# Quarter products, seven for eight, in the adjacency sweeps of a four-layer graph kernel

**The chip, the cores and the metric.** One core of one Trainium2 chip. The metric is device microseconds of one execution, as the median of the runs. A single core has no die to compare with, so a run is called fast when it is within 1.5% of the fastest of its kernel. In the profile's lines PE is TensorE's matmuls and PEld its weight loads, DVE is VectorE, ACT ScalarE, POOL GpSimd, and SPq the queue of SyncE, which issues loads; L102 is line 102 of that kernel.

## The reference

2708 nodes, 512 features, a dense f32 array `adj` that is mostly zeros. Four layers, each with a residual and a layer norm. Cut to what matters:

```python
# 0: inc = adj + mask / sqrt(row count of mask)
x = LN(x + (inc @ x) / rowsum(inc))
# 1: attention over adj's pattern, and a GCN, mixed by two gates
e = where(adj != 0, exp(-leaky_relu(s_left[:, None] + s_right[None, :])), 0)
x = LN(x + sigmoid(gate_a * (e / rowsum(e)) @ (x @ W_sa) + gate_b * (adj @ (x @ W_gcn) + b)))
# 2: three hops
x = LN(x + x W0 + A (x W1 + A (x W2 + A (x W3))))
# 3: pooled
x = LN(x + relu((((A x + x) / deg) + x) @ W + b))
```

So there are seven products of the form `adjacency @ features`, [2708 x 2708] by [2708 x 512].

## The kernel before

The adjacency lies transposed in DRAM. Its 128 x 128 blocks are the stationary operand, and 512 features move. All features stay in SBUF.

```python
def sweep_mm(ps, lhs, rhs, m, q, first=True, last=True):
    w = rows[m]
    k0, k1 = PIECES[q]
    for k in range(k0, k1):
        kr = rows[k]
        nc.tensor.matmul(ps[:w], lhs[q][:kr, k - k0, :w], rhs[k][:kr], start=first and k == 0,
                         stop=last and k == NT - 1)
```

The scale of layer 0's mask is a column of one row tile: a power on GpSimd, then a transpose on PE that spreads it.

```python
nc.vector.tensor_scalar(r[:w, 0:1], ps[:w], 1.0, None, ALU.max)
nc.gpsimd.tensor_tensor(r[:w, 1:2], r[:w, 0:1], neg_half[:w], ALU.pow)
# ... later
nc.tensor.transpose(r[:, 0, :w], scale[m][:w, 1:2].to_broadcast([w, P]), ident[:w, :w])
```

A hop is a sweep over a row tile and four dense matmuls for `x W` into the same PSUM bank; `x` is transposed again in each hop.

## Time and profile before

3712.6 us (3711.8 to 3713.6, three runs). The prediction below shows the page's shares, slices and chain.

### The profile page before, as it was taken

The page shows a single profiled execution, that of the slowest core. Times are in us where ns is not written, and L with a number is a line of the kernel's source. Part 1 is how long each engine was busy: PE and PEld are TensorE (multiplying, and loading weights), DVE is VectorE, ACT ScalarE, POOL GpSimd, SP SyncE. Part 2 cuts the span into 40 slices and gives each one's busy share as a digit, 9 for nine tenths or more (in the row PEclk, how much of TensorE's full clock was granted, in tenths as well). Part 3 has the DMA queues.
Part 4 walks back from the last instruction along what each step waited for, and adds up shares of the span by engine and source line. Part 5 has one row for each costly group of instructions (what it writes and reads, how often), then busy time and mean ns, then how long its engine had stood idle before and what let it go on. Part 6 is the DMA issues. An engine that isn't in the chain of part 4 may idle for free.

```text
span 3710.3 us, 25433 instructions
## 1 busy us (share of the span) xinstructions
PE 3679.8 (99%) x10340; PEld 1626.9 (44%) x10340; DVE 1057.5 (29%) x1807; ACT 265.2 (7%) x392; POOL 88.8 (2%) x249
## 2 busy tenths in 40 slices
PE   7999999999999999999999999999999999999999
PEld 3444444444444444344444434444344444344443
DVE  6676654444444444110000000000000001222222
ACT  0000001111111111110000000000000000000000
POOL 0000000000000000000000000000000000000000
PEclk9999999999999999999999999999999999999999
DMA  4222211111111110102222122222222221222220
GB/s 149 53 56 56 54 44 55 31 34 30 33 30 30 30 33 19 37 24 60 60 60 60 48 71 60 60 60 60 59 60 60 60 60 48 77 69 71 68 71 21
DMA packets 377865, 197.16 MB, mean 53 GB/s; under 512 B 27156, under 2 KB 368364, under 8 KB 377748
## 3 DMA queue, kind: packets, MB, share of 16 engines
q1 hardware_dynamic: 370278, 181.58, 18.8%
q10 hardware_dynamic: 7470, 13.95, 1.1%
q8 instruction: 82, 1.34, 0.1%
q14 instruction: 35, 0.29, 0.0%
HBM read 189.94 MB, written 5.55 MB: 53 GB/s over the span
## 4 chain that ended last, share of the span: by engine, by line
PE 99%; DMA 1%; DVE 0%; issue 0%; POOLq 0%; SPq 0%
PE acc L102 68%; PE ps_u L102 11%; PE acc L116 9%; PE ps_d L116 6%; PE ps_t L109 2%; PE ps_s L129 1%; PE ps_s L171 1%; PE ps_s L284 1%; PE ps_s L210 0%; DMA adj<-in_adjT 0%; DMA w<-in_w_hop 0%; PE ps_t L262 0%; PE ps_u L186 0%; DMA A<-in_x 0%; DVE tmp L192 0%; DVE y L380 0%
## 5 line engine op out<-in xcount | busy, mean ns | idle before, releaser
L102 PE MATMUL acc<-C,adj 128*128 128x512 f32 (+2 forms) x1936 | 855.4, 595 | 0.0
L102 PE MATMUL acc<-B,adj 128*128 128x512 f32 (+2 forms) x1936 | 853.5, 594 | 0.0
L102 PEld LDWEIGHTS acc<-B,adj 128*128 128x128 f32 (+2 forms) x1936 | 352.5, 186 | 462.3 <-issue 461.1
L102 PEld LDWEIGHTS acc<-C,adj 128*128 128x128 f32 (+2 forms) x1936 | 352.2, 186 | 462.7 <-issue 462.1
L102 PE MATMUL acc<-A,adj 128*128 128x512 f32 (+1 forms) x968 | 436.1, 600 | 2.3 <-DVE adj L194 2.3
L102 PE MATMUL acc<-C,edge 128*128 128x512 f32 (+1 forms) x968 | 436.0, 597 | 0.0
L102 PE MATMUL ps_u<-B,adj 128*128 128x512 f32 (+1 forms) x968 | 434.6, 595 | 0.0
L116 PE MATMUL acc<-w,xT 128*128 128x512 f32 (+1 forms) x704 | 324.7, 604 | 1.4 <-DMA w<-in_w_hop 1.4
L102 PEld LDWEIGHTS acc<-C,edge 128*128 128x128 f32 (+1 forms) x968 | 176.0, 185 | 248.0 <-issue 248.0
L111 ACT COPY xT<-ps_t 128x512 f32<-128x512 f32 (+1 forms) x154 | 87.7, 570 | 2748.9 <-PE ps_t L109 2741.6
L102 PEld LDWEIGHTS ps_u<-B,adj 128*128 128x128 f32 (+1 forms) x968 | 176.6, 186 | 229.3 <-issue 229.2
L102 PEld LDWEIGHTS acc<-A,adj 128*128 128x128 f32 (+1 forms) x968 | 174.2, 187 | 214.1 <-issue 195.6
L116 PE MATMUL ps_d<-w,xT 128*128 128x512 f32 (+1 forms) x528 | 243.5, 604 | 0.5 <-DVE y L380 0.5
L116 PEld LDWEIGHTS acc<-w,xT 128*128 128x128 f32 (+1 forms) x704 | 124.4, 186 | 182.6 <-issue 180.9
L358 DVE COPY C<-acc 128x512 f32<-128x512 f32 (+1 forms) x22 | 15.2, 692 | 494.2 <-PE acc L116 494.2
L358 DVE COPY B<-acc 128x512 f32<-128x512 f32 (+1 forms) x22 | 15.2, 691 | 494.2 <-PE acc L116 494.2
L116 PEld LDWEIGHTS ps_d<-w,xT 128*128 128x128 f32 (+1 forms) x528 | 92.8, 186 | 129.9 <-issue 128.4
L361 DVE TENSOR_TENSOR y<-acc,A 128x512 f32<-128x512 f32 (+1 forms) x22 | 15.2, 692 | 413.6 <-PE acc L116 413.4
L131 DVE TENSOR_SCALAR rd<-ps_s 128x1 f32<-128x1 f32 (+1 forms) x44 | 6.9, 157 | 431.2 <-PE ps_s L129 431.2
L122 DVE TENSOR_REDUCE part<-edge 128x128 f32<-128x768 f32 (+3 forms) x88 | 111.6, 1305 | 0.0
L122 DVE TENSOR_REDUCE part<-adj 128x128 f32<-128x768 f32 (+3 forms) x88 | 111.6, 1309 | 0.0
L372 DVE TENSOR_SCALAR edge<-adj 128x768 bf16<-128x768 f32 (+3 forms) x88 | 44.2, 509 | 208.4 <-PE ps_s L171 152.1
(72 smaller groups left out, 1477.5 us busy)
## 6 DMA issues: line engine op xcount, KB each, us to landing
adj<-in_adjT SPq DMA_DIRECT2D x252, 384.0 KB
adj<-in_adjT SPq DMA_DIRECT2D x126, 320.0 KB
adj<-in_adjT SPq DMA_DIRECT2D x126, 256.0 KB
A<-in_x ACTq DMA_DIRECT2D x21, 256.0 KB
out<-xa SPq DMA_DIRECT2D x21, 256.0 KB
w<-in_w_hop ACTq DMA_DIRECT2D x4, 1024.0 KB
adj<-in_adjT SPq DMA_DIRECT2D x126, 10.0 KB
w<-in_w_sa ACTq DMA_DIRECT2D x1, 1024.0 KB
```

Source lines behind the costliest of these rows:

```text
L102: nc.tensor.matmul(ps[:w], lhs[q][:kr, k - k0, :w], rhs[k][:kr], start=first and k == 0, stop=last and k == NT - 1)
L109: nc.tensor.transpose(ps[:, c, :w], src[:w, c * P : (c + 1) * P], ident[:w, :w])
L111: nc.scalar.copy(t[:, :, :w], ps[:, :, :w])
L116: nc.tensor.matmul(ps[:w], xT[:, c, :w], wt[:, c, :], start=first and c == 0, stop=c == DC - 1)
L122: nc.vector.tensor_reduce(s[:, :w], t[:, :nk, :w].rearrange("p k i -> p i k"), AX.X, ALU.add)
L129: nc.tensor.matmul(ps[:w], s[:, :w], ones, start=n == 0, stop=n == len(parts) - 1)
L131: nc.vector.tensor_scalar(rd[:w], ps[:w], eps, None, ALU.add)
L171: nc.tensor.matmul(ps[:w], mask[m][q][:, k - k0, :w], ones_bf, start=k == 0, stop=k == NT - 1)
L284: nc.tensor.matmul(pz[:w], xT[m][:, c, :w], wab_sb[:, c, :], start=c == 0, stop=c == DC - 1)
L358: nc.vector.tensor_copy(dst[m][:w], ps[:w])
L361: nc.vector.tensor_tensor(y[:w], ps[:w], x2[m][:w], ALU.add)
L372: nc.vector.tensor_scalar(t[:, : k1 - k0, :w], adj[m][q][:, : k1 - k0, :w], 0.0, None, ALU.not_equal)
```

## The change

Each adjacency is split into 2 x 2 quarters of 1354 rows and columns, each feature matrix into 2 x 2 quarters of 1354 rows and 256 features. Seven products of sums of quarters replace eight. Features become the stationary operand and adjacency rows move, 256 to 384 at a time, so the result comes out transposed. The rows of `x W` in a hop become two more contraction tiles of the sweep. Features now travel through DRAM between sweeps, and the order of everything is given by positions. The diff has 1161 lines; its core (comments and dots are mine):

```diff
-        nc.tensor.matmul(ps[:w], lhs[q][:kr, k - k0, :w], rhs[k][:kr], ...)
+STAT = dict(P1="B11", P7="T3", P5="T1", P6="T2", P2="B21", P4="T4", P3="B22")
+MOV = dict(P1="11", P7="s3", P5="21", P6="11", P2="12", P4="22", P3="12")
+            cw = {"s3": 0.3, "s1": 1.1, "s2": 2.1, "s4": 5.05}          # when the sums of pieces are made
+                nc.vector.tensor_tensor(A[r, dst, k][:w, :n], A[r, a, k][:w, :n], A[r, b, k][:w, :n], op)
+                for c in range(2):
+                    nc.tensor.matmul(B[home, c][:, :n], X[STAT[p], k][:w, c * P : (c + 1) * P],
+                                     A[r, MOV[p], k][:w, :n], start=bool(start and k == k0), stop=k == k1, ...)
 ... (cut)
-        nc.gpsimd.tensor_tensor(r[:w, 1:2], r[:w, 0:1], neg_half[:w], ALU.pow)
+    def count_row(R0, n, h):
+        t = trans("cr")
+        nc.vector.tensor_scalar(t[:, :n], cnt.pop(h)[:, :n], 1.0, None, ALU.max)
+        row[R0, h] = ring_tile("row")
+        nc.gpsimd.tensor_tensor(row[R0, h][:, :n], t[:, :n], neg_half.to_broadcast([P, n]), ALU.pow)
+    def prep0(r, R0, n, h, hj, k, a):                                   # adjacency piece -> inc piece
+        nc.vector.scalar_tensor_tensor(t[:w, :n], a[:w, :n], 0.0, row[R0, h][:w, :n], ALU.is_gt, ALU.mult)
+        nc.vector.tensor_tensor(a[:w, :n], a[:w, :n], t[:w, :n], ALU.add)
+        add_run(R0, h, n, w, a)
 ... (cut)
```

Adjacency rows now lie along the free dimension, so the mask's scale is wanted as a row of 256 to 384 elements, the same on all partitions.

## The prediction

> **What bounds the kernel now.** I first read the header of the page and the busy shares, then the slices, then the chain that ended last.
>
> ```profile
> span 3710.3 us, 25433 instructions
> PE 3679.8 (99%) x10340; PEld 1626.9 (44%) x10340; DVE 1057.5 (29%) x1807; ACT 265.2 (7%) x392; POOL 88.8 (2%) x249
> PE   7999999999999999999999999999999999999999
> DVE  6676654444444444110000000000000001222222
> PEclk9999999999999999999999999999999999999999
> PE 99%; DMA 1%; DVE 0%; issue 0%; POOLq 0%; SPq 0%
> ```
>
> PE idles 30 us in all (3710.3 - 3679.8), 22 of them before the first sweep matmul, and the mean granted clock is 0.999. So the time is the sum of PE's matmuls. VectorE has work in the first third and then almost none. To price a matmul I took the timeline of PE in a stretch of a hop (start, length, engine, line, operation, count):
>
> ```profile
> 1810.43 3.70 PE L116 MATMUL acc<-w,xT 128*128 128x512 f32 x8
> 1813.97 10.46 PE L102 MATMUL acc<-B,adj 128*128 128x512 f32 x24
> 1824.27 0.60 PE L109 MATMUL ps_t<-ident,A 128*128 128x128 f32 x4
> 1824.71 5.74 PE L102 MATMUL acc<-B,adj 128*128 128x512 f32 x13
> ```
>
> 24 records run from 1813.97 to 1824.27: 0.429 us each, start to start; four transposes take 0.44 us. Each f32 matmul leaves two records (a row tile has 22 blocks and shows 44), so one 512-column f32 matmul costs 0.858 us. The same reading elsewhere gives 0.112 us per record where only 1 or 2 columns move, and 0.025 us for a bf16 count matmul with one column. For VectorE I took its timeline in layer 0:
>
> ```profile
> 212.00 0.94 DVE L192 TENSOR_TENSOR tmp<-edge,ps_u 128x768 f32<-128x768 bf16 x1
> 212.85 1.82 DVE L194 TENSOR_TENSOR adj<-adj,tmp 128x768 f32<-128x768 f32 x2
> 200.16 0.75 DVE L200 SCALAR_TENSOR_TENSOR y<-acc,rd,A 128x512 f32<-128x512 f32 x1
> 200.94 0.69 DVE L137 BATCH_NORM_STATS2 st<-y 128x6 f32<-128x512 f32 x1
> ```
>
> Two independent f32 adds of 768 columns take 1.82 us where one takes 0.95: the second follows after 0.87[...]. One that needs the result of the one before starts 0.03 us after its end (200.16 + 0.75, then 200.94)[...].
>
> [...]
>
> **The sweeps, PE.** Before: 7 products with the adjacency in 6 streams (layer 1 does two), 22 x 22 matmuls of 512 columns each: 3388 x 0.858 = 2907 us. In addition blocks of 20 rows cost some 0.1 us more per record (0.533 and 0.517 against 0.429) and so does one neighbour, 0.29 us x 154 row tiles = 44 us. After: a quarter product has 11 tiles of contraction (10 of 128, one of 74 rows), two halves of 128 features as stationary, and 1354 adjacency rows as moving columns in pieces of 384, 384, 256 and 330. One (tile, half) over the four pieces: [...] 2275 ns. 7 products x 22 = 154 of these per sweep, 350.4 us, against 415 + 6. Seven sweeps: 2453 us, 498 less. Only 8/7 of that is the algorithm; the rest is that 2708 rows are no longer padded to 22 full tiles on both sides. [...]
>
> **Hops' dense rows.** Removed: 3 x 22 x 4 matmuls, 264 x 0.858 = 227 us. Added: two more contraction tiles per quarter, 3 x 7 x 4 x 2275 ns = 191 us.
>
> **The rest of PE.** Unchanged in number: 352 dense matmuls (302 us), 616 transposes (67 us at 0.109; those saved by recomputing x2's once are spent on turning results back), 176 gate matmuls (39 us). Row sums fall from 176 matmuls to 44 (39 to 10 us). Degrees: 484 one-column counts remain (12 us); layer 0's become 176 matmuls with 338 columns on average, 143 ns each, 25 us for 12.
> Sum after: 2453 + 191 + 302 + 67 + 39 + 10 + 12 + 25 = 3099 us. The same sum for before is 2907 + 44 + 529 + 67 + 39 + 39 + 24 + 6 (wide transposes) = 3655; with 30 us idle, 3685 against a span of 3710, 0.7% short. Scaled by 3680/3655, after has 3120 us of PE work. With before's idle that would be 3150, 15% off; what remains is how much more PE will wait.
>
> **Where PE will wait.** By widths 384, 384, 256, 330 an independent f32 operation costs VectorE 420 ns on average, a chained one 535. Each sweep gets 176 sums of adjacency pieces (74 us), 11 x 4 sums of features (17), 40 additions that leave PSUM (18): 109 us, harmless beside 425 to 460 us of PE. Two sweeps have element work besides. Layer 0: 176 pieces x (two chained + one independent) = 176 x 1.49 = 262 us, layer norm with its waits on GpSimd 22 x 4.1 = 90, small ones 6: 467 us, against PE's 350 + 25 + 19 + 20 + 5 = 420. VectorE becomes the bound of this sweep. It also starts later: 22 pieces are read and run through two ACT instructions each (about 0.4 us for 256 columns, from ACT's 843 ns at 768 and 737 at 640) before the first row count, so the first sweep matmul comes at about 32 us, not 22. The last part of the sweep needs no more element work. I put its end near 505 us: 32 of start and 55 of VectorE above PE's own time. Attention sweep: 262 + 109 + 22 x 3.9 + 7 = 464 us of VectorE against PE's 350 + 151 + 15 = 516; unevenly spread, 15 us of waits. Six joints between sweeps: the last row tiles go through transpose, layer norm and copy (5 us for one, some 10 for three) before the last three contraction tiles can run; the change places these late in the first product, so I take 5 us each, with the half-speed matmuls that follow a gap (four records at twice their time after the one at 1561 us): 30. PSUM hand-overs at 28 range ends: 10 together. The end: last additions, pooling, layer norm, store: 12 us not beside PE.
> 3120 + 32 + 55 + 15 + 30 + 10 + 12 = 3274; the events of the change are placed with evident care against just these waits, so I shade this to **3260 us** (ratio 0.878).
>
> **Rivals.** (1) VectorE takes over in both element sweeps and in-order queues spread it: its waits for GpSimd (power of a whole row count, 256 to 384 columns, whose cost no row shows; layer norm queued behind DMA issues waiting for a buffer)[...]. For: 467 against 420 us; against: 29% DVE before, and nothing like it in the other five sweeps. It would make 3350 to 3420. (2) Buffers: adjacency, its sums and all temporaries share 44 slots, of which 44 are in use where the third product starts; in-order loads then come late, a few us in each of 28 ranges. 3300 to 3350. For: SyncE already waited mostly for PE to free buffers; against: the loads are issued half a product (7 us) ahead or more, and one issue takes 0.37 us. (3) DMA: traffic rises from 197 to about 350 MB as seven streams, re-read counts and features through DRAM, 107 GB/s on average. Against: the first slice of before moved 149 GB/s with 512-byte pieces, at four tenths busy. No effect. (4) Everything hides: 3120 + 30 to 60, 3150 to 3180. Against it speaks the start, which nothing hides.
>
> **Range and chances.** The PE sum is firm to 1%: its unit costs are the trace's. Waits can hardly be under 70 us nor, with rivals 1 and 2 together, much over 240: 3195 to 3350. To lose the whole gain would take 450 us more of waiting; faster by over 2% has 0.97.
>
> **What would show it.** About 11,716 matmul records (2 x 5220 f32 + 616 + 484 + 176). The 384-column records 322 ns apart, 330 at 277, 256 at 216; wider gaps would refute the PE sum, above all on tiles of 74 rows. DVE near 9 tenths in the first 500 us and 8 in the attention sweep, 2 to 4 in the hops; PE at 8 or less in the first five slices and at full in the hops. If PE there stays at 9, rival 4 holds; if PE has gaps in every range waiting for DMA, rival 2; if the first sweep lasts beyond 560 us with DVE waiting for POOL, rival 1. [...] PE below 93% outside the first sweep, would make the prediction wrong.

The sum came to 3274 us and was shaded to 3260. What the formulas priced were my estimates for widths that the kernel before does not have, and "its unit costs are the trace's" holds only for the widths that it has; the changed kernel's trace now shows the others. Its f32 records of 384, 330 and 256 columns start 322, 277 and 216 ns apart, so one (tile, half) takes 2 x (322 + 322 + 277 + 216) = 2274 ns (2275 above). Its count matmuls of 384 and 330 columns start 162 and 140 ns apart (143 above, an average over all widths). Two-input VectorE operations that do not wait for each other start 469, 412 and 335 ns apart at 384, 330 and 256 columns, 421 on average (420 above); where one needs the result of the one before, 583 at 384 and 527 at 330 (535 above, an average). That a matmul with 74 rows costs the same as one with 128 was an assumption (325 ns a record were measured, against 322.5), and the 15, 30, 10 and 12 us of waits in the sum were my estimates (36 us were measured, not 67). The first records after the gap at 1561 us start 0.85 to 1.02 us apart, against 0.43 later, in the kernel before.

## More of the kernel before

By stage, from the view that sums a stretch of time (stretch in us; its length; busy us and instructions of PE, weight loads, VectorE, ACT and GpSimd; granted clock; DMA share; GB/s); the stretches are layer 0, layer 1, the dense product that opens layer 2, the three hops, and layer 3:

```profile
0.00:584.00 584.00, 564.44 (x2075) 269.95 (x2076) 373.58 (x634) 25.90 (x43) 29.11 (x74) 1.00 0.25 68
584.00:1561.00 977.00, 977.00 (x2601) 434.10 (x2601) 442.97 (x683) 176.69 (x239) 17.66 (x44) 1.00 0.12 32
1561.00:1645.00 84.00, 79.99 (x242) 38.89 (x241) 17.62 (x28) 12.46 (x22) 0.54 (x1) 0.98 0.04 13
1645.00:3169.00 1524.00, 1524.00 (x3687) 651.16 (x3687) 82.10 (x156) 37.60 (x66) 24.62 (x86) 1.00 0.23 60
3169.00:3710.30 541.30, 534.32 (x1741) 232.79 (x1739) 141.21 (x308) 12.54 (x22) 16.85 (x44) 1.00 0.23 64
```

The second figure of a line is the length and the third is PE's busy time: PE has next to no idle time in any stage, so each stage lasts as long as its matmuls.

## The result

3664.7 us (3657.1 to 3668.2, four runs), against 3712.2 of the kernel before. The ratio is 0.987 (95% interval 0.9855 to 0.9883). A ratio here is the mean time of one kernel's fast runs over that of the other's of the same rounds, so not quite the ratio of the medians. I had predicted 3260.

The page of the changed kernel: header, busy shares, slices of PE, GpSimd and PE's clock, the first line of the chain, and one line of the costliest groups (line, engine, operation, operands, count, busy us, mean ns, idle time before it):

```profile
span 3662.9 us, 34944 instructions
PE 3187.2 (87%) x11716; PEld 2055.3 (56%) x11716; DVE 1652.4 (45%) x4077; ACT 564.6 (15%) x1118; POOL 776.3 (21%) x604
PE   2433637549999999999999999999999999999998
POOL 6485572572100000111121000200011101120000
PEclk9776867769999999999999999999999999999999
PE 70%; issue 3%; DVE 2%; DMA 1%; POOL 1%; ACT 0%; POOLq 0%; SPq 0%; DVEq 0%
L418 POOL TENSOR_TENSOR row<-cr,neg_half 128x384 f32<-128x384 f32 (+2 forms) x8 | 435.3, 54409 | 135.9 <-DVE cr L416 98.2
```

PE's work is down from 3680 to 3187 us, as hoped. But the first ten slices, the first sweep, are half empty, GpSimd is busy there and little elsewhere, and PE's clock falls to 0.6 to 0.8 in most of them. The last line is the new thing: eight powers of 54 us on average, 435 us in all. They took 41.2 us for 256 columns, 53.1 for 330 and 61.6 for 384, some 161 ns per column. By stage, as above (layer 0; layer 1 with the opening product of layer 2; hops; layer 3):

```profile
0.00:910.90 910.90, 471.42 (x1761) 305.34 (x1762) 405.22 (x1085) 171.52 (x395) 510.28 (x146) 0.78 0.38 95
910.90:1884.30 973.40, 965.25 (x3734) 602.63 (x3733) 568.77 (x1502) 303.45 (x536) 101.36 (x173) 0.99 0.38 101
1884.30:3213.70 1329.40, 1317.16 (x4789) 876.95 (x4788) 469.27 (x1015) 77.21 (x159) 139.49 (x244) 1.00 0.40 115
3213.70:3662.90 449.20, 433.41 (x1437) 270.37 (x1435) 209.16 (x479) 12.37 (x28) 25.19 (x42) 0.98 0.35 102
```

Outside layer 0 the change saved 88 us (1061 to 973), 195 us (1524 to 1329) and 92 us (541 to 449): 374 us. PE idles 36 us there in all. Layer 0 lost 327 us (584 to 911), with PE idle for 439 of its 911. A stretch of a hop shows PE as predicted (start, length, then the instruction and how many):

```profile
2499.80 1.46 PE L283 MATMUL accc<-s,T 74*128 74x384 f32 x4
2501.10 2.75 PE L283 MATMUL accc<-s,e 128*128 128x384 f32 x8
2503.68 4.68 PE L283 MATMUL accd<-a,T 128*128 128x384 f32 x14
```

Eight records of 384 columns from 2501.10 to 2503.68 are 0.3225 us each, and the four with 74 rows 0.325.

What one power does, in the timelines of GpSimd and VectorE of layer 0 (in brackets the idle time before, and what ended it):

```profile
260.82 61.74 POOL L418 TENSOR_TENSOR row<-cr,neg_half 128x384 f32<-128x384 f32 x1 [3.13 <-DMA a<-in_adjT]
322.55 0.54 POOL L343 TENSOR_TENSOR rstd<-rstd,neg_half 128x1 f32<-128x1 f32 x1
```

```profile
265.01 0.55 DVE L430 SCALAR_TENSOR_TENSOR s<-a,row 128x384 f32<-128x384 f32 x1
323.13 0.55 DVE L345 TENSOR_SCALAR o<-ld,mv,rstd 128x512 f32<-128x512 f32 x1 [57.57 <-POOL rstd L343]
```

VectorE works for some five us beside the power, meets a layer norm whose own small power (0.54 us) stands behind the long one in GpSimd's queue, and then waits 57.6 us. And in the waits of SyncE's load queue (who waited for whom; us in total, times, longest):

```profile
SPq L405 <- POOL row L418: 194.6, 4, 60.1
SPq L240 <- POOL row L418: 63.9, 1, 63.9
```

So a load also waits for a power. That must be for its slot in the shared pool, as a load of the adjacency needs no result of GpSimd. The loads behind it wait too: SyncE issued one at 496.48 us, the next at 560.89, when the power that began at 499.29 had ended, and the one after that at 561.32. Three ways from one instruction to a stop, then: the row is wanted; something else stands behind it in the queue; its tile holds a slot that the load queue wants next. A fourth would be that VectorE's operations do not run while a power does. I call this the lockout; it was a suspicion that no trace had shown.

### The profile page after: what moved, and what is told of

It is laid out like the page before. It is cut to its first block, busy times and chain, and to the rows that moved or that the text cites. A ratio compares the mean times of both kernels' runs of the same rounds, so it can differ in the third digit from the quotient of the medians.

```text
span 3662.9 us, 34944 instructions
## 1 busy us (share of the span) xinstructions
PE 3187.2 (87%) x11716; PEld 2055.3 (56%) x11716; DVE 1652.4 (45%) x4077; ACT 564.6 (15%) x1118; POOL 776.3 (21%) x604
## 4 chain that ended last, share of the span: by engine, by line
PE 70%; issue 3%; DVE 2%; DMA 1%; POOL 1%; ACT 0%; POOLq 0%; SPq 0%; DVEq 0%
PE accu L283 18%; PE accc L283 17%; PE accd L283 17%; PE acca L283 9%; PE ps_d L381 7%; PE ps_n L367 1%; POOL B L177 1%; PE ps_t L373 0%; PE pz L587 0%; DMA B<-Y 0%; POOL rstd L343 0%; DVE T L158 0%; PE deg L563 0%; DVE run L425 0%; DMA B<-X 0%
## 5 line engine op out<-in xcount | busy, mean ns | idle before, releaser
L250 DVE TENSOR_TENSOR a<-a,a 128x384 f32<-128x384 f32 (+4 forms) x988 | 484.6, 507 | 255.6 <-DMA a<-in_adjT 110.2
L418 POOL TENSOR_TENSOR row<-cr,neg_half 128x384 f32<-128x384 f32 (+2 forms) x8 | 435.3, 54409 | 135.9 <-DVE cr L416 98.2
L283 PE MATMUL accu<-a,B 128*128 128x384 f32 (+5 forms) x1232 | 401.1, 467 | 40.9 <-DVE a L431 40.9
L283 PE MATMUL acca<-a,B 128*128 128x384 f32 (+5 forms) x1232 | 376.1, 459 | 38.3 <-DVE a L431 38.3
L283 PE MATMUL accc<-s,T 128*128 128x384 f32 (+5 forms) x1232 | 375.4, 460 | 9.7 <-DVE s L250 9.7
L283 PE MATMUL accd<-a,B 128*128 128x384 f32 (+5 forms) x1232 | 380.4, 455 | 0.0
L283 PE MATMUL accd<-a,T 128*128 128x384 f32 (+5 forms) x1232 | 362.1, 449 | 0.3 <-DVE a L250 0.3
L283 PE MATMUL accu<-a,T 128*128 128x384 f32 (+5 forms) x1232 | 360.1, 448 | 0.0
L283 PE MATMUL accc<-a,T 128*128 128x384 f32 (+5 forms) x1200 | 353.7, 451 | 0.0
L283 PEld LDWEIGHTS accc<-s,T 128*128 128x128 f32 (+1 forms) x1232 | 234.5, 194 | 126.4 <-DVE s L250 16.5
```

The source lines that it names most:

```text
L250: nc.vector.tensor_tensor(A[r, dst, k][:w, :n], A[r, a, k][:w, :n], A[r, b, k][:w, :n], op)
L283: nc.tensor.matmul(B[home, c][:, :n], X[STAT[p], k][:w, c * P : (c + 1) * P], A[r, MOV[p], k][:w, :n], start=bool(start and k == k0), stop ...
L418: nc.gpsimd.tensor_tensor(row[R0, h][:, :n], t[:, :n], neg_half.to_broadcast([P, n]), ALU.pow)
```

## The experiments

Theory: the powers are the whole miss, by the first three ways. Rivals: VectorE's element work bounds layer 0 (my prediction), or the lockout. All runs were correct, except one.

**e1: the power elsewhere.**

```diff
-        nc.gpsimd.tensor_tensor(row[R0, h][:, :n], t[:, :n], neg_half.to_broadcast([P, n]), ALU.pow)
+        nc.vector.reciprocal(t[:, :n], t[:, :n])
+        nc.scalar.activation(row[R0, h][:, :n], t[:, :n], AF.Sqrt)
```

> The change, with the eight row powers of layer 0 taken from GpSimd and computed as a VectorE reciprocal and an ACT square root. Theory (the eight 41 to 62 us powers are the whole miss): PE's eight gaps of 37 to 57 us (365 us together) go, the first sweep falls from 911 to 500-560 us, the other six stay at 2752 +- 15 us, total 3240 to 3320. Rival VectorE (the first sweep is slow because of the amount of element work, the powers only stand beside it): first sweep stays above 700, total above 3450. Rival lockout [...]: same total as the theory here, told apart by e2 and e7.

Measured: 3290.1 us, ratio 0.886 (0.8846 to 0.8876) to the kernel before. Its page (header, shares, PE's slices), then its first sweep in the view by stretch:

```profile
span 3287.5 us, 34930 instructions
PE 3165.9 (96%) x11716; PEld 2043.4 (62%) x11716; DVE 1665.9 (51%) x4085; ACT 570.4 (17%) x1128; POOL 341.4 (10%) x596
PE   4988999999999999999999999999999999999998
```

```profile
0.00:535.00 535.00, 449.28 (x1760) 292.89 (x1761) 418.06 (x1092) 175.92 (x404) 74.99 (x138) 0.95 0.65 161
```

The first sweep takes 535 us instead of 911, and the other six 2752.5 instead of 2752.0. In place of a power, a reciprocal ran on VectorE: 1.75 us for 256 columns and up to 2.55 for 384 (e8's trace). The powers cost 375 us, nearly the 365 us of the eight long gaps of PE, and without them the total lies inside the range that I had predicted. Of the difference in the first sweep 354 us are idle time of PE (439 against 86) and 22 are busy time, with a mean granted clock of 0.78 against 0.95. That left the question how one instruction costs that much, and I guessed badly at it.

**e2, e3, e7: one way at a time.** e2 has the fast row of e1 and lets GpSimd compute the power in place, unread. e3 keeps the slow row and takes layer 0's layer norm off GpSimd. e7 does both. In e2's text "such operations" are VectorE's with two inputs.

```diff
 e2:
-        nc.gpsimd.tensor_tensor(row[R0, h][:, :n], t[:, :n], neg_half.to_broadcast([P, n]), ALU.pow)
+        nc.vector.reciprocal(row[R0, h][:, :n], t[:, :n])
+        nc.scalar.activation(row[R0, h][:, :n], row[R0, h][:, :n], AF.Sqrt)
+        nc.gpsimd.tensor_tensor(t[:, :n], t[:, :n], neg_half.to_broadcast([P, n]), ALU.pow)
 e3, in layer 0's layernorm:
-        nc.gpsimd.tensor_tensor(rstd[:w, 1:2], rstd[:w, 0:1], neg_half[:w], ALU.pow)
+        nc.vector.reciprocal(rstd[:w, 0:1], rstd[:w, 0:1])
+        nc.scalar.activation(rstd[:w, 1:2], rstd[:w, 0:1], AF.Sqrt)
```

> As e1, but GpSimd still computes the eight powers, in place, and nobody reads them. Theory A (only the wait for the row counts): as e1, 3240 to 3320. Theory B (what stands behind the power in GpSimd's queue, the layer norms' own small powers and feature loads, counts too): some of the eight gaps stay, 3400 to 3560. Lockout: [...] total 3600 or more. In the trace after the change such operations ran at their usual 0.41 us inside the first power after one of 0.72, so I expect B.

> The change with its row powers on GpSimd as they are, but layer 0's layer norm computed without GpSimd (VectorE reciprocal, ACT square root). Theory A: the waits for the rows stay, 3620 to 3680. Theory B: the three VectorE waits of 48 to 58 us for a small power behind a row power go (161 us), and part of them comes back as waits for the row: 3500 to 3600.

> Both: fast rows, powers on GpSimd that nobody reads, layer norm off GpSimd. If only the row waits and the norms behind the powers cost time: as e1, within 60 us (feature loads still queue behind the powers). Lockout: well above e1, by up to 435 us, the sum of the powers.

Measured: e2 3669.0, e3 3629.3, e7 3588.1 us. e2 missed the 3400 to 3560 that I expected. e3 fell where I had put theory A, in which only the waits for the rows count, and e7 where I had put the lockout. A power that nobody reads costs as much as one that everybody waits for, and with the norm off GpSimd as well it still costs 298 us. By my own words 3600 or more in e2 spoke for the lockout, too: numbers alone would have convicted it. The waits of SyncE's queue in e7 named another suspect:

```profile
SPq L409 <- POOL cr L424: 150.2, 3, 63.1
SPq L240 <- POOL cr L424: 53.4, 1, 53.4
```

The unread power still holds the count's tile, which is one of the 44 slots.

**c1, e8, e9, e10: the tile out of the pool.** In all four the count's tile has two buffers of its own, and the pool 42 slots.

```diff
-RING = 44
+RING = 42
-        t = trans("cr")
+        t = pool.tile([P, 384], F32, name="cr", tag="cr", bufs=2)
```

c1 is e1 so edited (the control), e8 is e7, e9 is e2, e10 is e3.

> Control for the next three: fast rows as in e1, but the row-count tile has two buffers of its own and the shared pool 42 slots instead of 44. Expected as e1, 3290 within 30 us; if the two slots matter, more.

> As e7 (fast rows, powers unread, layer norm off GpSimd), but the power works in place on a tile outside the shared pool. In e7 the in-order load queue of SyncE waited 204 us for the power to give its slot back, and the load is then the head of everything. Theory slot: this coupling is the 298 us by which e7 exceeds e1, so here 3290 to 3370 (the first feature loads still stand behind the first power, about 35 us). Lockout or GpSimd's time as such: unchanged near 3590.

> As e2 (fast rows, powers unread, layer norm on GpSimd), with the power's tile outside the pool. Only the small powers of the layer norm wait behind the long ones: three to five waits of 40 to 58 us, total 3400 to 3560. If the queue of GpSimd does nothing, as c1; if the slot was not the cause, 3669.

> As e3 (the powers are read, layer norm off GpSimd), with the count's tile outside the pool: only the wait for the row itself is left. Rows are asked for about as far ahead as the count ends before the first piece, less than a power's 41 to 62 us, so eight waits of 20 to 45 us: 3480 to 3640.

Measured: c1 3297.5, e8 3463.6, e9 3609.7, e10 3591.9 us. c1 and e10 came as expected; e9 lies above its range, and e8 between its two theories. The two slots cost 7 us, about the spread of c1's own runs. The slot was real: e7 to e8 gains 124 us. But 166 us were left in e8, more than I allowed for. One wait carries the verdict in each of e10, e9 and e8 (layer 0, in this order):

```profile
DVE s L434 <- POOL row L422: 306.8, 7, 50.3
```

```profile
DVE o L345 <- POOL rstd L343: 282.5, 18, 60.9
```

```profile
SPq L390 <- DMA X<-o: 152.0, 6, 50.7
```

In e10 VectorE waits for the row itself: 307 us, against a loss of 294 over the control. In e9 nobody reads the row and no slot is held, and VectorE waits 282 us for small powers of the layer norm behind the long ones; the loss is 312. In e8 neither is left, and SyncE's fetches wait 152 us for stores of finished features. GpSimd issues those, so they stand behind the power too: one was issued at 378.14 us, as the power of 61.55 us that began at 316.63 ended. About the lockout, GpSimd and VectorE in e8, at the same time:

```profile
316.63 61.55 POOL L424 TENSOR_TENSOR cr<-cr,neg_half 128x384 f32<-128x384 f32 x1
```

```profile
332.45 0.55 DVE L436 SCALAR_TENSOR_TENSOR s<-a,row 128x384 f32<-128x384 f32 x1
333.44 0.55 DVE L437 TENSOR_TENSOR a<-a,s 128x384 f32<-128x384 f32 x1
334.45 0.55 DVE L431 TENSOR_TENSOR run<-run,a 128x384 f32<-128x384 f32 x1
```

Two-input VectorE operations run inside the power at 0.55 us, as they do outside it.

**e12: nothing behind the powers.** e8, with layer 0's stores and first feature loads issued by ACT.

```diff
-                store(X1[t], o, w)
+                store(X1[t], o, w, nc.scalar)
-                    nc.gpsimd.dma_start(out=SROW[R0, h]...
+                    nc.scalar.dma_start(out=SROW[R0, h]...
-        at(-0.8 + f, lambda k=k: x_load(X0, k, "B21", nc.gpsimd))      # and B22, B12
+        at(-0.8 + f, lambda k=k: x_load(X0, k, "B21", nc.scalar))
```

> As e8, with the feature stores, score rows and first feature loads of layer 0 issued by ACT instead of GpSimd, so that nothing that the sweep needs stands behind the powers. If queue and slot are the whole cost of a long GpSimd instruction: as the control c1 (3297), within 40 us. If e8's remaining 166 us were lockout or some share of GpSimd itself: 3400 or more.

Measured: 3292.4 us, against 3297.5 of the control. In GpSimd's timeline the powers still run, now almost without a pause:

```profile
62.89 58.34 POOL L424 TENSOR_TENSOR cr<-cr,neg_half 128x256 f32<-128x256 f32 x1
122.66 258.22 POOL L424 TENSOR_TENSOR cr<-cr,neg_half 128x384 f32<-128x384 f32 x4 [1.43 <-DVE row L422]
```

They cost next to nothing. c1 is not quite the control for e12, as the issues and the layer norm moved too: e12's first sweep matmul starts at 27.8 us, c1's at 39.9. But from there to the end of the sweep e12 takes 505.7 us and c1 503.9. And 258 VectorE additions of 384 columns, in the first sweep and wholly inside a power, took 0.549 us on average in e12; in c1, without powers, 269 took 0.550. This closes the account: what a long GpSimd instruction costs here is what waits for it, and the lockout of VectorE is refuted as a cause.

The other way round, three powers ran longer beside VectorE's work. e12's second power (above, at 62.89) took 58.3 us, where one of this width takes 41.2. From before its start VectorE ran two-input operations without any gap up to this one, at 80.2:

```profile
79.82 0.41 DVE L437 TENSOR_TENSOR a<-a,s 128x256 f32<-128x256 f32 x1
81.06 0.43 DVE L250 TENSOR_TENSOR s<-a,a 128x256 f32<-128x256 f32 x1 [0.83 <-PE accc L283]
```

From the gap to the end of the power are 41.0 us. The two powers of 384 columns that are over 10 us longer than the others, one in e12 (71.7 us) and one in e8 (73.1), show the same: their last 61.4 and 61.5 us begin where VectorE's run of such operations first breaks. From there on each of the three took as long as an undisturbed power of its width (41.2 and 61.6 us); what held it up before is not shown. Also, one VectorE operation at or near the start of most powers takes 0.3 to 0.8 us longer (in the changed kernel 1.07 us for 384 columns at 261.18 and 1.19 for 330 at 736.70, against 0.55 and 0.50).

| kernel | row waited for | norm behind | tile in the pool | stores, loads behind | us |
|---|---|---|---|---|---|
| the change | yes | yes | yes | yes | 3664.7 |
| e2 | | yes | yes | yes | 3669.0 |
| e3 | yes | | yes | yes | 3629.3 |
| e9 | | yes | | yes | 3609.7 |
| e10 | yes | | | yes | 3591.9 |
| e7 | | | yes | yes | 3588.1 |
| e8 | | | | yes | 3463.6 |
| e12 | | | | | 3292.4 |
| e1, no powers | | | | | 3290.1 |

The ways do not add up: taking the tile out of the pool gains 124 us from e7 to e8, 59 from e2 to e9 and 37 from e3 to e10. As I read it, they stand side by side behind the same instruction, and the longest that is left decides, so one change at a time had to look as if little helped.

**e4: the eighth product put back.** e1, with P2 computed twice; the second pass starts afresh, so the result is right.

```diff
+                if p == "P2":
+                    for a in (False, True):
+                        for k in ks:
+                            at(pb + i + 0.5 * a + 0.5 * k / nk, ... step("P2", k, o[0], o[-1], again=a))
```

> As e1, with the product P2 computed twice (the second time from a fresh start, so the result is right): PE's work of 8 products of quarters. 664 more matmuls, 7 x 22 + 3 x 4 = 166 of them per set of pieces at 2.275 us: 378 us. If PE is the bound outside the first sweep and nearly so inside, 3640 to 3670; if the first sweep hides it behind other engines, some 50 less.

Measured: 3658.3 us, 368 more than e1. The eighth product is worth 368 us of the 422 by which e1 beats the kernel before (3712.1 - 3290.1), at 97% of the PE time counted for it. With eight products of quarters (e4) the gain over the kernel before is only 1.5%.

**e11: less work for VectorE.** e1 without the running sums of layer 0's pieces (wrong result, relative error 0.16; 1 is added to each row sum so that none is zero).

> As e1, but layer 0's pieces are not added up for the row sums (wrong result on purpose): 168 VectorE operations of about 0.42 us fewer, 70 us of VectorE in the first sweep. My prediction made VectorE the bound of that sweep: then 40 to 70 us faster than e1. Rival: what is left of the gaps comes from the start, late layer norms and loads: 0 to 20 us faster.

Measured: 3281.6 us, 9 less than e1; the first sweep takes 524 us against 535, with VectorE busy 350 us against 418:

```profile
0.00:524.30 524.30, 451.99 (x1761) 296.08 (x1762) 350.18 (x943) 177.95 (x404) 75.16 (x138) 0.94 0.67 164
```

So the amount of VectorE's work does not bound the first sweep.

**e13: an attempt to improve on e1.**

```diff
-            at(p + 0.5, c)
-            at(p + 0.65, d)
+            at(p + 0.9, c)
+            at(p + 1.05, d)
+        if R0 == RANGES0[0][0] and h == 0 and i % 2:
+            nc.vector.tensor_scalar(m[:w, :n], t[:w, :n], 0.0, None, ALU.is_gt)
```

> Attempt at a better version: e1 with layer 0's transposes of finished rows placed 0.4 product later in the order (PE waited 25 us in seven gaps for the layer norm in e1), and half of the first count's comparisons on VectorE, idle there, instead of two ACT passes. 3250 to 3280; if the gaps only move, 3290.

Measured: 3300.4 us. It is 10 us slower than e1; the first sweep took 548 us in its trace. The gaps moved: PE's waits for the layer norm fell from 25.5 to 4.4 us, those for VectorE's sums and pieces rose from 13 to 25 and those for the counts from 46 to 55. Two things were changed at once, and 9 or 10 us between runs of different sessions (e11, e13) are near the limit of what can be told. e1 stays the best kernel.

## Why the prediction was wrong

**The PE sum held.** 11,716 records were predicted and found. Records of 384 columns are 322 to 323 ns apart against 322 predicted, and tiles of 74 rows carry no penalty (0.325 us a record against 0.3225). In e1 PE was busy 3166 us against 3120 predicted. Its mean granted clock was 0.986, and 0.95 in the first sweep; that of the kernel before was 0.999. I take part of the 46 us to be this; how much is not shown.

**The time outside the first sweep held.** The prediction's sum left 3274 - 505 = 2769 us for the other six sweeps with their joints and the end. The trace has 2752. PE idles 36 us there, the end included, where the sum had 67 (15 + 30 + 10 + 12), so the waits there were put too high.

**The step that failed is the one for the first sweep:** "I put its end near 505 us: 32 of start and 55 of VectorE above PE's own time." It measured 911. The term that was missing is the power of a whole row, eight times 41 to 62 us. It was priced at nothing in the sum. Rival 1 names it, "power of a whole row count, 256 to 384 columns, whose cost no row shows", and still allows the whole rival no more than 160 us (3420 - 3260); the powers cost 375 (e1). The sign that the prediction set for this rival, a first sweep beyond 560 us with VectorE waiting for GpSimd, came true: in the changed kernel VectorE waited 181 us for the layer norm's small powers and 84 for the rows. The kernel before shows a GpSimd power only on one column, 0.55 us. That bounds a row of 384 only to between 0.55 and 211 us (384 x 0.55, an estimate). Eight at the upper end would be more than the whole gain. An open cost of that size belongs in the range and not in a rival. The range I gave, 3195 to 3350, holds e1 (3290), the change without its powers.

**VectorE as the bound of the first sweep was wrong too, but hidden.** e11 takes some 70 us of its work away and gains 9. Its busy time in e1 is 418 us, not 467: the schedule puts another piece's operation between two dependent ones, so I should not have charged the price of a chain (583 ns for 384 columns in the changed kernel, against 469). The 535 us of e1's first sweep came close to 505 for other reasons, which is luck. The first sweep matmul starts at 40 us, not 32, and PE then waits in fifteen more gaps of 1.5 to 7 us. With the shorter ones, PE's waits from there on are 25 us for layer norms, 15 for counts and 13 for VectorE's sums and pieces; e13 did not settle which of these binds.

**Of the rivals,** 2 (buffers) was right about the pool and wrong about the culprit: what holds a slot too long is not a load but GpSimd. 3 (DMA) was not tested: traffic rose to 383 MB, at 105 GB/s on average, and the experiments account for the miss without it, but in e1's first 40 us the DMA engines were 0.89 busy at 274 GB/s, so part of the late start may be theirs. 4 (everything hides) nearly came true outside the first sweep (36 us idle in 2752).

## What to carry to other kernels

Before an operation is moved to another layout, count its elements per partition on its engine. If the profile shows that operation only at one element (0.55 us here), its cost at 384 is unknown (it was 61.6), and a range must say so. A long GpSimd instruction cost next to nothing by itself here (e12, 3292.4 us against 3297.5); it cost what stood behind it, what read it, and whoever next wanted the buffer it held. Where several of these lead to the same stop, removing them one at a time shows little, so remove the instruction first and then put the ways back.
